# Score products on four array quarters, unread products at the start, and two stores per half group in a four-layer graph network

## The chip, the cores and the metric

The kernel runs on one core of a Trainium2 chip. The metric is the device time of one execution in microseconds (us). The program is one launch; nothing is computed on the host but the layout of the inputs.

## The reference

The input `x` holds 128 graphs of 64 nodes with 256 features; one 64x64 adjacency matrix serves them all. Four layers follow, each `x = x + layer(relu(layernorm(x)))`. Cut to what matters:

```python
# layer 0: two graph convolutions, then four LSTMs over windows of 1, 2, 3, 4 nodes
h = relu(adj @ (h @ Wg0 + bg0));  h = relu(adj @ (h @ Wg1 + bg1))
for p in 1..4: h[:, last node of each window of p] = lstm_p(windows of h)
# layer 1: spectral mix, then attention with 4 heads of 64, then an MLP
x1 = relu(layernorm((2 L / lam_max - I) @ h @ Wc + bc)) + h
q, k, v = x1 @ Wq, x1 @ Wk, x1 @ Wv            # 4 heads of 64
attn = softmax(where(adj > 0, q @ k.T / 8, -1e9))
x2 = layernorm(x1 + (attn @ v) @ Wo + bo)
x = layernorm(x2 + gelu(x2 @ W1 + b1) @ W2 + b2)
# layer 2: graph attention; layer 3: U @ (relu(U.T @ h @ W1 + b1) @ W2 + b2)
# lam_max and U come from eigenvalues and eigenvectors of 64x64 matrices
```

In layer 1 a score product is 64x64 times 64x64: one graph, one head. There are 128 x 4 of them, and as many products of probabilities and values.

## The kernel before

**Tiles.** The 128 graphs are 64 token tiles of 128 rows (two graphs each). Layer 0 goes over 8 groups of 8 tiles, layers 1 to 3 over 16 half groups of 4 tiles (`HT = 4`, 8 graphs). Features are cut into two chunks of 128 (`c`, `m`); in feature-major form a chunk holds two heads, one on partitions 0-63 and one on 64-127. All data is fp32, and each fp32 product appears in the trace as two records.

**Order.** The code records operations without emitting them (`Plan.record`). `Plan.schedule` then simulates the engines with a fixed cost per operation (`Plan.cost`), picks buffers and PSUM banks, and writes out one order for every engine. Groups have numbers: setup first, then layer 0 group by group, a set of weights loaded into the room of layer 0's weights, then the half groups of layers 1 to 3, of which several are open at once. The eigenvector work (`eig_decomp` and what follows it) is a group of its own beside layer 0: its TensorE products go ahead of all others, the rest of it behind. All records have the same line, 331, where `Plan.issue` emits; so groups are read by tiles and shapes.

**TensorE's cost in the plan.** A transpose is taken at 0.11 us, a product of at most 64 by 64 at 0.08, all others at 0.001672 us per column plus 0.006, and no less than 0.06. A list of products under `plan.burst()` is planned as one operation, at 0.3 us plus 0.036 for each product; both bursts of layer 1 have 32.

**Layer 1's two bursts.** `qT` and `kT` are feature-major: chunk `m`, and in it partition half `r`, is head `2m + r`. A score product has its contraction on the 64 partitions of half `r`. Its place in the 128x128 array is given by the half of the partitions that it reads (array rows) and the half of the partitions that it writes (array columns). Before, the scores of a head land on the partition half that the head is read from:

```python
for par, m, b in [(r, r ^ f, b) for f in range(2) for b in range(2 * HT) for r in (f, 1 - f)]:
    r = slice(par * N, par * N + N)
    PE.matmul(ps[m][r, bat(b)], qT[r, m, bat(b)], kT[r, m, bat(b)], start=True, stop=True)
```

So only the two straight quarters (0-63 to 0-63, 64-127 to 64-127) are used in each of the two passes `f`, and neighbouring products go to different banks `ps[0]`, `ps[1]`. Mask, softmax and transposes follow, on `s` and `pT`. The second burst multiplies by `v`: the graph's half of the tokens (`half`) is read, the head's half (`par`) written, in all four combinations, each half of the tokens into a bank of its own.

**The start.** `ident` and `ones` are set on chip. The first loads are `adjT`, `adj` and five pieces of `x`. Two products with `adjT` give row sums (`rsrow`), for bias tables. Then layer 0 of group 0 begins: statistics, normalised tiles `mids`, products with `adjTb`, copy, products with `Wg`.

**The end of a half group.** `layer3` adds its result to `x` in two halves of two tiles, and one store on the SyncE queue writes the four tiles (512 KB) to the output.

Of the kernel before, what the change touches and what calls it, by code (L numbers as in the profile page):

```python
# [12 lines left out]
N = 64  # L13
# [53 lines left out]
class Plan:  # L67
# [101 lines left out]
    @staticmethod  # L169
    def cost(op, aps):  # L170

        def free(ap):
            n = 1
            for _, c in ap.ap[1:]:
                n *= c
            return n
        n = max(free(a) for a in aps)
        if op.name == "dma_start" and op.eng != "SP":
            return 0.6, 4.0
        if op.eng == "PE":  # L180
            n = free(aps[0])
            if op.name == "transpose":
                c = 0.11
            elif aps[0].ap[0][1] <= 64 and aps[1].ap[0][1] <= 64:
                c = 0.08
            else:
                c = max(0.06, 0.001672 * n + 0.006)
            return c, c + 0.22
        if op.eng == "V":
            if op.name == "bn_stats":  # L190
                c = 0.33
            elif op.name == "bn_aggr":
                c = 0.09
            elif op.name in ("tensor_copy", "tensor_scalar") and all(str(a.space) == "SB" for a in aps):
                c = 0.075 + 0.0006 * n + 0.05 * (len(aps) - 2)
            elif op.name == "reciprocal":
                c = 0.075 + 0.0065 * n
            elif op.name == "tensor_reduce" and aps[1].ap[-1][0] != 1:
                c = 0.075 + 0.0022 * n
            else:  # L200
                c = 0.075 + 0.00105 * n
            if "accum_out" in op.kw:
                c += 0.075
            return c, c + 0.12
        if op.eng == "ACT":
            c = 0.07 + 0.00082 * n + 0.1 * max(0, len(aps) - 2)
            if op.kw.get("func", op.args[2] if len(op.args) > 2 else None) is AF.Exp:
                c += 0.12
            return c, c + 0.15
        if op.eng == "G":  # L210
            c = 0.44 + 0.14 * n if op.kw.get("op") is ALU.pow else 0.12 + 0.00218 * n
            return c, c + 0.05
        c = max(0.6, free(aps[0]) * aps[0].ap[0][1] * 4e-6 / 0.39)
        return c, c + 2.2
# [650 lines left out]
P = 128  # L865
D = 256
NT = 64
GT = 8
NG = NT // GT
HT = 4  # L870
# [41 lines left out]
def gnn_kernel(ctx: ExitStack, tc: tile.TileContext, a, out):  # L912
# [4 lines left out]
    def C(shape, name):  # L917
        return pool.tile(list(shape), F32, name=name)
# [40 lines left out]
    PE, V, ACT, G, SP = (plan.proxy(e) for e in ("PE", "V", "ACT", "G", "SP"))  # L959

    def bank(name):
        return plan.value("bank")
# [11 lines left out]
    xout = out.rearrange("(g t p) f -> g p t f", p=P, t=HT)  # L974
# [38 lines left out]
    V.tensor_scalar(ident, ident, 0.0, None, op0=ALU.is_equal)  # L1013
    ones = C([P, P], "ones")
    V.memset(ones, 1.0)
    mhalf = C([P, HT], "mhalf")
    V.memset(mhalf, -0.5)

# [100 lines left out]
    bat = lambda b: slice(b * N, (b + 1) * N)  # L1119

    def tm(n=HT, f=D):

        return plan.value("big")[:, :n * f].rearrange("p (t f) -> p t f", f=f)

    def fm():

        return plan.value("big")[:, :2 * HT * P].rearrange("p (c n) -> p c n", c=2)
# [168 lines left out]
    def evac(dst, src, i):  # L1296
        if i % 2:
            ACT.copy(dst, src)
        else:
            V.tensor_copy(dst, src)  # L1300
# [36 lines left out]
    def relu_norm(x):  # L1337
        sc, bi = ln_stats(x)
        h = tm()
        for t in range(HT):  # L1340
            ACT.activation(h[:, t, :], x[:, t, :], AF.Relu, scale=sc(t), bias=bi(t))
        return h
# [11 lines left out]
    def layer1(x):  # L1354
        h = relu_norm(x)
        lx = mix_fm(h, lambda t: lapb)
        x1 = tm()
        for t0 in (0, 2):
            ps = proj_tm(lambda c, t: lx[:, c, tok(t)], Wc, 2, t0)
            V.tensor_add(x1[:, t0:t0 + 2, :], ps.rearrange("p (t f) -> p t f", t=2), vec(bc, 2))  # L1360
        norm(x1)
        for t0 in (0, 2):
            xp, hp = x1[:, t0:t0 + 2, :], h[:, t0:t0 + 2, :]
            V.tensor_mul(xp, xp, vec(g1, 2))
            G.tensor_add(xp, xp, vec(be1, 2))
            V.scalar_tensor_tensor(xp, xp, 0.0, hp, op0=ALU.max, op1=ALU.add)
        x1T = to_fm(x1)
        qT, kT, v = fm(), fm(), tm()
        for m in range(2):
            evac(qT[:, m, :], proj_fm(Wq, x1T, m), 0)  # L1370
            evac(kT[:, m, :], proj_fm(Wk, x1T, m), 1)
        for t0 in (0, 2):
            evac(pair(v, t0), proj_tm(lambda c, t: x1T[:, c, tok(t)], Wv, 2, t0), 1)
        for t0 in (0, 2):
            G.tensor_add(x1[:, t0:t0 + 2, :], x1[:, t0:t0 + 2, :], vec(bo, 2))

        ps = [bank("qk") for m in range(2)]
        with plan.burst():  # L1380
            for par, m, b in [(r, r ^ f, b) for f in range(2) for b in range(2 * HT) for r in (f, 1 - f)]:
                r = slice(par * N, par * N + N)
                PE.matmul(ps[m][r, bat(b)], qT[r, m, bat(b)], kT[r, m, bat(b)], start=True, stop=True)
        s = tm(4 * HT, N)
        for m in range(2):
            sm = s[:, m * 2 * HT:(m + 1) * 2 * HT, :]
            V.scalar_tensor_tensor(sm, ps[m].rearrange("p (b k) -> p b k", k=N), 0.125, vec(mask1, 2 * HT), op0=ALU.mult, op1=ALU.add)
            stat = plan.value("stat")
            softmax_shift(sm, stat[:, :2 * HT])
            ACT.activation(sm, sm, AF.Exp)  # L1390
            ssum = stat[:, 2 * HT:4 * HT]
            V.reduce_sum(ssum, sm, axis=AX.X)
            V.reciprocal(ssum, ssum)
            G.tensor_mul(sm, sm, ssum.unsqueeze(2).to_broadcast([P, 2 * HT, N]))

        pT = fm()
        for m in range(2):
            evac(pT[:, m, :], transposes([flat(s[:, (m * HT + t) * 2:(m * HT + t) * 2 + 2, :]) for t in range(HT)]), m)
        oT = fm()

        po = [bank("o") for half in range(2)]
        with plan.burst():
            for m, t, half, par in [(m, t, half, par) for m in range(2) for t in range(HT) for half in range(2) for par in range(2)]:
                r = slice(half * N, half * N + N)
                PE.matmul(po[half][par * N:par * N + N, bat(m * HT + t)], v[r, t, bat(2 * m + par)], pT[r, m, bat(2 * t + par)], start=True, stop=True)
        for half in range(2):
            evac(oT.rearrange("p c (t b n) -> p c t b n", t=HT, b=2)[:, :, :, half, :], po[half].rearrange("p (c t n) -> p c t n", c=2, t=HT), half)
        x2 = tm()
        for t0 in (0, 2):
            ps = proj_tm(lambda c, t: oT[:, c, tok(t)], Wo, 2, t0)  # L1410
            V.tensor_add(x2[:, t0:t0 + 2, :], ps.rearrange("p (t f) -> p t f", t=2), x1[:, t0:t0 + 2, :])
        norm(x2)
        x2T = fm()
        for c in range(2):
            ACT.activation(x2T[:, c, :], transposes([x2[:, t, tok(c)] for t in range(HT)]), AF.Identity, scale=g2c[:, c:c + 1], bias=be2c[:, c:c + 1])
        V.tensor_mul(x2, x2, vec(g2))
        for t0 in (0, 2):
            G.tensor_add(x2[:, t0:t0 + 2, :], x2[:, t0:t0 + 2, :], vec(b2, 2))
        mT = [fm() for i in range(2)]
        for m in range(4):  # L1420
            ACT.activation(mT[m // 2][:, m % 2, :], proj_fm(W1, x2T, m), AF.Gelu, bias=b1[:, m:m + 1])
        for t0 in (0, 2):
            ps = proj_tm(lambda c, t: mT[c // 2][:, c % 2, tok(t)], W2, 4, t0)
            V.tensor_add(pair(x2, t0), ps, pair(x2, t0))
        for t0 in (0, 2):
            G.tensor_add(x[:, t0:t0 + 2, :], x[:, t0:t0 + 2, :], vec(be3, 2))
        norm(x2)
        for t0 in (0, 2):
            V.tensor_mul(x2[:, t0:t0 + 2, :], x2[:, t0:t0 + 2, :], vec(g3, 2))
            V.tensor_add(x[:, t0:t0 + 2, :], x[:, t0:t0 + 2, :], x2[:, t0:t0 + 2, :])  # L1430
# [55 lines left out]
    for i, g in enumerate(ORDER):  # L1486
        plan.group = REST + 2 * i
        x = X[g]
        if g < len(put):
            x = load(back[g], put[g])  # L1490
        for h in range(GT // HT):
            plan.group = REST + 2 * i + h
            xh = x[:, h * HT:(h + 1) * HT, :]
            layer1(xh)
            layer2(xh)
            layer3(xh)
            SP.dma_start(xout[g * GT // HT + h], xh)
    plan.issue()


# [51 lines left out]
```

## Time and profile before

Three runs took 2292.06, 2292.18 and 2292.21 us.

| what | value |
|---|---|
| span of the profiled execution | 2291.3 us |
| TensorE busy | 2254.4 us |
| VectorE busy | 1693.3 us |
| ScalarE busy | 969.8 us |
| GpSimd busy | 565.7 us |
| mean granted TensorE clock | 0.996 |
| table loads on ScalarE | 43, of 1.283 us each |
| stores to the output | 16 of 512 KB, median 2.9 us from issue to landing |

How to read it: busy time is the union of an engine's instructions. Where an engine is busy nearly all the time, the end moves with its work. Where it idles, the question is what it waits for. The granted clock says at which share of full speed TensorE ran. A row of the timeline gives the start, the length, the engine and the operation with its count; in square brackets stands the idle time before it and what ended it. The length of a TensorE row ends with its last product's modelled end, which overlaps the next row; the time that a row takes up is from its start to the next row's start.

### The profile page before, as it was taken

How to read it: one execution, taken by the hardware profiler on the slowest of the kernel's cores; microseconds unless marked ns; L12 is line 12 of the kernel's file. 1: busy time of each engine (PE TensorE's matmuls, PEld its weight loads, DVE VectorE, ACT ScalarE, POOL GpSimd, SP SyncE). 2: the span in 40 equal slices, each digit the busy share in tenths (PEclk: the TensorE clock that was granted, in tenths of full speed). 3: DMA queues.
4: the chain of work that ended last, by engine and by line, in shares of the span. 5: the costliest groups of instructions: out<-in, count | busy, mean ns of one | idle time of the engine just before them, and what ended most of it. 6: DMA issues, size and time to landing. Idle time of an engine off the chain costs nothing.

```text
span 2291.3 us, 33480 instructions
## 1 busy us (share of the span) xinstructions
PE 2254.4 (98%) x11288; PEld 1595.1 (70%) x11288; DVE 1693.3 (74%) x6942; ACT 969.8 (42%) x1909; POOL 565.7 (25%) x856
## 2 busy tenths in 40 slices
PE   8999999999999999999999999999999999999997
PEld 5578478468568568568568558778777776876786
DVE  6656666566899999999988723767786867767775
ACT  3333333333333333333333443455564545555672
POOL 3101001101100100100100203535374535555342
PEclk9999999999999999999999999999999999999998
DMA  7000001000000000000000011000000000000001
GB/s 247 1 1 19 0 1 38 19 1 1 1 1 1 1 1 1 1 1 1 5 1 1 9 36 31 1 1 10 20 10 10 10 28 10 28 10 1 2 19 37
DMA packets 27405, 35.48 MB, mean 15 GB/s; under 512 B 3297, under 2 KB 24673, under 8 KB 26721
## 3 DMA queue, kind: packets, MB, share of 16 engines
q1 hardware_dynamic: 26128, 32.29, 4.2%
q8 instruction: 89, 1.46, 0.3%
q10 hardware_dynamic: 1104, 1.05, 0.2%
q14 instruction: 84, 0.68, 0.1%
HBM read 22.85 MB, written 10.49 MB: 15 GB/s over the span
## 4 chain that ended last, share of the span: by engine, by line
PE 91%; DVE 5%; ACT 2%; POOL 1%; issue 1%; DMA 0%; SPq 0%; DVEq 0%; ACTq 0%
PE bank L331 91%; DVE arena L331 2%; DVE big L331 1%; DVE stat L331 1%; DVE x L331 1%; POOL stat L331 1%; ACT big L331 1%; DVE mids L331 0%; ACT arena L331 0%; ACT L331 0%; ACT mids L331 0%; ACT Wih L331 0%; DMA adj<-in_adj_dram 0%; ACT x L331 0%; DVE Whh L331 0%
## 5 line engine op out<-in xcount | busy, mean ns | idle before, releaser
L331 PE MATMUL bank<-big,Wih 128*128 128x512 f32 (+2 forms) x2640 | 887.6, 478 | 2.2 <-DVE arena L331 1.1
L331 PEld LDWEIGHTS bank<-big,Wih 128*128 128x128 f32 x2640 | 490.0, 190 | 275.3 <-issue 172.4
L331 ACT ACTIVATE mids<-bank,bl 128x256 f32<-128x256 f32 (+2 forms) x624 | 345.2, 563 | 637.0 <-PE bank L331 622.3
L331 PE MATMUL bank<-big,Whh 128*128 128x256 f32 (+3 forms) x1640 | 507.3, 444 | 0.0
L331 DVE TENSOR_TENSOR arena<-arena 64x21 f32<-64x21 f32 (+6 forms) x2316 | 375.9, 193 | 34.7 <-POOL arena L331 1.8
L331 PEld LDWEIGHTS bank<-big,Whh 128*128 128x128 f32 x1640 | 306.4, 190 | 132.4 <-issue 65.5
L331 POOL TENSOR_SCALAR stat<-stat 128x4 f32<-128x4 f32 (+1 forms) x228 | 67.5, 297 | 722.4 <-DVE stat L331 709.7
L331 DVE TENSOR_TENSOR big<-big,mids 128x256 f32<-128x256 f32 (+2 forms) x192 | 93.8, 489 | 123.7 <-ACT mids L331 122.3
L331 DVE TENSOR_TENSOR big<-mids 128x512 f32<-128x512 f32 (+2 forms) x256 | 145.9, 574 | 47.0 <-ACT mids L331 43.5
L331 ACT ACTIVATE mids<-big 128x256 f32<-128x256 f32 (+2 forms) x176 | 89.8, 510 | 99.6 <-DVE big L331 64.8
L331 PE MATMUL bank<-Wih,big 128*128 128x256 f32 (+1 forms) x560 | 130.2, 365 | 0.2 <-ACT big L331 0.2
L331 DVE TENSOR_SCALAR arena<-arena 64x1 f32<-64x1 f32 (+4 forms) x598 | 120.3, 210 | 8.2
L331 POOL TENSOR_TENSOR arena<-arena 64x1 f32<-64x1 f32 x66 | 43.6, 661 | 322.6 <-ACT arena L331 170.2
L331 POOL TENSOR_TENSOR stat<-stat,mhalf 128x4 f32<-128x4 f32 (+1 forms) x114 | 120.4, 1057 | 6.5
L331 PEld LDWEIGHTS bank<-Wih,big 128*128 128x128 f32 x560 | 97.6, 190 | 21.9 <-issue 10.7
L331 PE MATMUL bank<-Whh,big 128*128 128x256 f32 (+2 forms) x512 | 110.2, 358 | 1.4 <-DVE x L331 1.0
L331 ACT COPY big<-bank 128x512 f32<-128x512 f32 x113 | 63.0, 587 | 111.5 <-PE bank L331 94.1
L331 PEld LDWEIGHTS bank<-Whh,big 128*128 128x128 f32 (+1 forms) x512 | 82.3, 183 | 21.9 <-issue 8.3
L331 DVE COPY arena<-bank 64x1 f32<-64x1 f32 (+24 forms) x190 | 41.2, 220 | 71.4 <-PE bank L331 64.9
L331 PEld LDWEIGHTS bank<-adjTb,mids 128*128 128x128 f32 x512 | 69.8, 193 | 25.7 <-issue 17.0
L331 DVE BATCH_NORM_STATS2 stat<-x 128x6 f32<-128x256 f32 x240 | 87.2, 410 | 0.1
L331 ACT ACTIVATE mids<-x,stat 128x256 f32<-128x256 f32 x92 | 48.4, 591 | 88.2 <-POOL stat L331 88.2
(334 smaller groups left out, 3313.1 us busy)
## 6 DMA issues: line engine op xcount, KB each, us to landing
x<-in_x_dram SPq DMA_DIRECT2D x7, 1024.0 KB, 13.2
out_dram<-x SPq DMA_DIRECT2D x12, 512.0 KB, 2.9
Wih<-in_WihT_dram SPq DMA_DIRECT2D x3, 1024.0 KB, 15.7
Whh<-in_WhhT_dram SPq DMA_DIRECT2D x3, 1024.0 KB, 12.2
put<-x SPq DMA_DIRECT2D x2, 1024.0 KB, 4.4
arena<-put SPq DMA_DIRECT2D x2, 1024.0 KB, 5.9
out_dram<-arena SPq DMA_DIRECT2D x4, 512.0 KB, 3.0
Whh<-in_W_dram SPq DMA_DIRECT2D x2, 512.0 KB, 3.8
```

The lines of the kernel that those rows point to most:

```text
L331: getattr(self.engines[op.eng], name)(*map(real, args), **{k: real(a) for k, a in kw.items()})
```

## The change

It has four parts.

1. The score products of the second chunk (`m = 1`) write the other partition half (`half(r ^ m)`), so the four products of a graph lie in the four quarters of the array. They are issued graph by graph: chunk 0 with both halves into bank 0, then chunk 1 with both halves into bank 1. The second burst reads the probabilities of the second chunk at swapped places.
2. Fourteen products of `ones` with itself, 128x128, whose result nobody reads, are recorded at the beginning of the program, where TensorE has no data yet.
3. The output of a half group is stored in two halves of 256 KB.
4. The plan takes 0.2 us for a product of fewer than 128 columns, if it isn't a transpose or at most 64 by 64. The formula for wider ones stays.

```diff
             elif aps[0].ap[0][1] <= 64 and aps[1].ap[0][1] <= 64:
                 c = 0.08
             else:
-                c = max(0.06, 0.001672 * n + 0.006)
+                c = 0.001672 * n + 0.006 if n >= 128 else 0.2
...
     V.memset(ones, 1.0)
+
+    warm = bank("warm")
+    for i in range(14):
+        PE.matmul(warm[:, :P], ones, ones, start=True, stop=True)
...
         ps = [bank("qk") for m in range(2)]
+        half = lambda i: slice(i * N, i * N + N)
         with plan.burst():
-            for par, m, b in [(r, r ^ f, b) for f in range(2) for b in range(2 * HT) for r in (f, 1 - f)]:
-                r = slice(par * N, par * N + N)
-                PE.matmul(ps[m][r, bat(b)], qT[r, m, bat(b)], kT[r, m, bat(b)], start=True, stop=True)
+            for b, m, r in [(b, m, r) for b in range(2 * HT) for m in range(2) for r in range(2)]:
+                PE.matmul(ps[m][half(r ^ m), bat(b)], qT[half(r), m, bat(b)], kT[half(r), m, bat(b)], start=True, stop=True)
...
-            for m, t, half, par in [(m, t, half, par) for m in range(2) for t in range(HT) for half in range(2) for par in range(2)]:
-                r = slice(half * N, half * N + N)
-                PE.matmul(po[half][par * N:par * N + N, bat(m * HT + t)], v[r, t, bat(2 * m + par)], pT[r, m, bat(2 * t + par)], start=True, stop=True)
+            for m, t, i, r in [(m, t, i, r) for m in range(2) for t in range(HT) for i in range(2) for r in range(2)]:
+                PE.matmul(po[i][half(r), bat(m * HT + t)], v[half(i), t, bat(2 * m + r)], pT[half(i), m, bat(2 * t + (r ^ m))], start=True, stop=True)
...
-            SP.dma_start(xout[g * GT // HT + h], xh)
+            for t0 in range(0, HT, 2):
+                SP.dma_start(xout[g * GT // HT + h][:, t0:t0 + 2, :], xh[:, t0:t0 + 2, :])
```

More of the change, by code (lines that the diff above doesn't have):

```diff
@@ L1399, in layer1 @@
         oT = fm()
-        po = [bank("o") for half in range(2)]
+        po = [bank("o") for i in range(2)]
         with plan.burst():
-            for m, t, half, par in [(m, t, half, par) for m in range(2) for t in range(HT) for half in range(2) for par in range(2)]:
-                r = slice(half * N, half * N + N)
-                PE.matmul(po[half][par * N:par * N + N, bat(m * HT + t)], v[r, t, bat(2 * m + par)], pT[r, m, bat(2 * t + par)], start=True, stop=True)
-        for half in range(2):
-            evac(oT.rearrange("p c (t b n) -> p c t b n", t=HT, b=2)[:, :, :, half, :], po[half].rearrange("p (c t n) -> p c t n", c=2, t=HT), half)
+            for m, t, i, r in [(m, t, i, r) for m in range(2) for t in range(HT) for i in range(2) for r in range(2)]:
+                PE.matmul(po[i][half(r), bat(m * HT + t)], v[half(i), t, bat(2 * m + r)], pT[half(i), m, bat(2 * t + (r ^ m))], start=True, stop=True)
+        for i in range(2):
+            evac(oT.rearrange("p c (t b n) -> p c t b n", t=HT, b=2)[:, :, :, i, :], po[i].rearrange("p (c t n) -> p c t n", c=2, t=HT), i)
         x2 = tm()
```

## The prediction

> **What bounds the kernel now.** I read the page from its top: busy shares, the 40 slices, the chain that ended last. Then the timeline of TensorE where the edited instructions stand, and a table of stretches for how full TensorE is around them.
>
> ```profile
> PE 2254.4 (98%) x11288; PEld 1595.1 (70%) x11288; DVE 1693.3 (74%) x6942; ACT 969.8 (42%) x1909; POOL 565.7 (25%) x856
> PE   8999999999999999999999999999999999999997
> PE 91%; DVE 5%; ACT 2%; POOL 1%; issue 1%; DMA 0%; SPq 0%; DVEq 0%; ACTq 0%
> ```
>
> TensorE is busy in 98% of the span, in every slice but the first and the last, and 91% of the chain is its work. VectorE (74%) is next, with room. So nearly every microsecond of TensorE work removed comes off the end, and nearly every one added goes on.
>
> The two bursts of 64x64 products come next. Each fp32 product stands in the trace as two records, so 32 products are x64. One half group's scores (columns: start, duration, engine, operation, count) and another's values times probabilities, each with the row that follows:
>
> ```profile
> 2128.41 2.08 PE L331 MATMUL bank<-mids,big 64*64 64x64 f32 x64
> 2130.42 1.13 PE L331 MATMUL bank<-Whh,arena 128*128 128x256 f32 x4
> 2131.48 1.16 PE L331 MATMUL bank<-big,x 64*64 64x64 f32 x64
> 2132.57 1.13 PE L331 MATMUL bank<-Whh,arena 128*128 128x256 f32 x4
> ```
>
> From a burst's start to the next row's start: 2130.42 - 2128.41 = 2.01 us for the first kind, 2132.57 - 2131.48 = 1.09 us for the second, with equal work in them. Which is which follows from the code: the first 64x64 burst of the kernel, at 1458.74, has the long form, and scores come first; the last, at 2163.28, has the short one. The code also says why they differ: the scores before run in two quarters of the array at any time (rows 0-63 to columns 0-63 together with rows 64-127 to columns 64-127, then the two crossed quarters), the values in all four. Sixteen of each stand in the trace.
>
> How full TensorE is there (columns: stretch and length, busy us and count per engine, granted clock, DMA):
>
> ```profile
> 20.00:1458.00 1438.00, 1434.19 (x5538) 966.46 (x5537) 1075.02 (x5208) 517.37 (x1121) 155.56 (x280) 1.00 0.04 13
> 1458.00:2020.00 562.00, 553.28 (x4006) 419.72 (x4008) 420.04 (x1134) 299.22 (x534) 286.69 (x383) 1.00 0.04 13
> 2020.00:2230.00 210.00, 210.00 (x1449) 158.67 (x1442) 151.65 (x427) 128.22 (x209) 96.53 (x130) 1.00 0.02 6
> ```
>
> From 1458 to 2230 us, where all score bursts stand, TensorE idles 8.7 us of 772 (562.00 - 553.28), and none of it after 2020. VectorE works 420.0 of 562 and 151.7 of 210, so it is no second bound yet.
>
> The head, and the end of the tail:
>
> ```profile
> 9.35 2.14 PE L331 MATMUL bank<-adjTb,mids 128*128 128x128 f32 x8 [1.97 <-ACT mids L331]
> 12.17 3.47 PE L331 MATMUL bank<-Wg,mids 128*128 128x256 f32 x8 [0.68 <-ACT mids L331]
> ...
> 2286.12 1.29 DVE L331 TENSOR_TENSOR arena<-bank,arena 128x512 f32<-128x512 f32 x2 [1.72 <-PE bank L331]
> ```
>
> Eight records of 256 columns take 3.47 us (0.43 each) at 12.17; twelve take 2.81 us (0.23) at 22.47. The first ones ran at half clock. The trace states the same later, with clock 0.50 granted after TensorE had idled:
>
> ```profile
> 2233.85:2237.26 3.41, 0.82 (x8) 0.64 (x7) 3.41 (x10) 0.94 (x3) 0.00 (x0) 1.00 0.00 0
> 2237.30:2244.00 6.70, 6.03 (x28) 5.62 (x28) 4.11 (x16) 3.61 (x7) 4.69 (x9) 0.50 0.00 0
> ```
>
> **What the Trainium skill says.** "TensorEngine Tiling (Array Packing)", section Tile-to-Partition Mapping: the array splits into four 64x64 tiles, each tied to one half of the input and one half of the output partitions. The trace agrees: four quarters 1.09 us, two 2.01. "PSUM — Partial Sum Buffer", section on bank collisions: two row tiles may not write the same bank at one time; what was measured is an error per bank and quadrant of 32 partitions, and the hardware does not stall for it. This matters, since after the change rows 0-63 and rows 64-127 write one bank together, but always in different partition halves: the page's measured rule allows it, its quoted general rule doesn't. In the trace of before two row tiles never share a bank within a burst, so it shows neither. "TensorE: Matmul & The Clock Gate", Part 1: the clock is halved until about 3.4 us of sustained work, and again after an idle window; the trace agrees (above). "DMA: Bandwidth & Descriptors", Anatomy of one DMA: about 2.0 us fixed plus bytes at 436 GB/s, stated for another issuing path than this one. For 512 KB that is an estimate of 3.2 us; the trace has 2.9.
>
> **The change, part by part.**
>
> *Scores.* 32 products per half group as before, now four in flight. I take the value burst's 1.09 us as their duration, as it has the same shapes, count and four quarters: 2.01 - 1.09 = 0.92 us per burst, times 16 = 14.7 us. The values burst itself only reads its operands at swapped places for the second pair of heads: no cost. Does the saving reach the end? TensorE idles 1.1% of that stretch, so mostly; where it runs ahead of VectorE's or ScalarE's fixed order some of it becomes a wait. I take 14.0.
>
> *Fourteen unread products.* They read `ones`, set by VectorE at 0.99 us. They are 28 records at half clock: 0.21 us each (half of the 0.43 of a record twice as wide) to 0.27 (2.14 / 8), so 6.0 to 7.5 us, less if the clock rises on the way. TensorE's queue has 12 of them, then the product of `adjT` and `ones` (at 3.15 before), two more, then the one with `rscol` (6.70 before), which then waits until at most about 9. Its reader is VectorE's copy `rsrow`, at 9.01 before; behind that in VectorE's queue stand the small bias tables, and the next TensorE work at 9.35 does not need them. So they cost nothing to 0.2 us. Their gain: 2.14 us of records, and about 3 of the 3.47, ran at half clock; at full clock they take half, so at most 2.6 us. But between the unread products' end (6 to 7.5) and 9.35 TensorE is idle but for two records, and 0.82 us of work in 3.41 was followed by a halved clock at 2237. I expect the clock to be lost again in part of the cases. Bounds 0 and 2.6; I take 0.8.
>
> *Two stores.* The last store is issued at 2287.44, when both of VectorE's last additions are done; 512 KB land in 2.9 us. After it, the first half leaves one addition earlier (0.65 us, half of 1.29) and the last is of 256 KB. By the trace, 1024 KB took 4.4 and 512 KB 2.9, so 256 KB less is 0.75 us less; by the page's rate it is 0.6. I take 0.7. The sixteen extra issues cost 0.37 us each on a queue that waits most of the time; only two loads stand behind stores there, long before they are needed.
>
> *The planner's cost.* Products of under 128 columns are now planned at 0.2 us instead of 0.06 to 0.11. No instruction changes, but the written order does, from the first microseconds on. The listing of both programs' instructions by engine shows the same kinds of work but 49 table loads on ScalarE for 43 (1.28 us each in the trace, 7.7 us on an engine at 42%), and the last 846 products of TensorE in the same order of shapes: from about 2020 us on, the tail is as it was. Up to 1458 TensorE idles 3.8 us of 1438 after the head: little to win there, little to lose if the order stays as good. Between 1458 and 2020 it idles 8.7 us, and a new order can make that 5 or 14. I take 0, with 4 us either way.
>
> Sum: 14.0 + 0.8 + 0.7 = 15.5; 2292.2 - 15.5 = 2276.7 us.
>
> **The rivals.**
>
> *A, given back (2285 us).* The bursts shorten, but half of it goes into waits on VectorE and ScalarE, whose order is fixed and now has six more table loads: 6 x 1.28 = 7.7 us if all six stand in front of TensorE. For it: TensorE waited 4.6 us for `Wih` from ScalarE, waits that contain table loads. Against: between 2020 and 2230 it idles not at all. 2276.7 + 7.7 = 2284.4, about 2285.
>
> *B, no overlap gained (2291 us).* Rows 0-63 and 64-127 in one bank hold each other up, so two of the four run at a time, as before: 2.01 us stay. Only head and tail remain: 2292.2 - 1.5 = 2290.7. For it: the page's quoted rule. Against: its measured one.
>
> *C, slower (2320 us).* The four products run one at a time. Two quarters take 2.01 us, so one takes about twice the streaming part: the four to two step costs 0.92 us for 16 slots, the two to one step 32 slots, 1.84 us. Times 16 = 29.4; with B's 2290.7 that is 2320.1. A badly placed new order would end on this side too. Against: in the trace the crossed quarters of the scores already alternate row tiles without that cost.
>
> **How the numbers follow.** Forecast 0.70, A 0.15, B 0.08, C 0.07. The forecast's own spread: 14.7 fully realised, 2.6 at the head and 4 from order would make 2270; I go to 2269 below. Above, 2290 takes in A and nearly reaches B; that holds all but about 0.05 of the forecast, most of A and some of B: 0.8. Faster by over 0.2% means below 2287.6: the forecast with A, less what of A falls above, 0.84. Within: B and that rest, 0.09. Slower: C, 0.07.
>
> **What would show it.** Right: the score bursts' next row starts 1.1 us after them, sixteen times; TensorE's busy time falls by 14 to 15 us while its idle time between 1458 and 2230 stays near 8.7; the records at 9.35 take about half of 2.14 us or the full; the last store lands about 2.2 us after its issue. Wrong: bursts of 2.0 us (B) or 3.9 (C); idle time in the middle grown by over 5 us (A); or TensorE waits before 1458 that were not there.

## The result and the profile after

Six runs of the changed kernel took 2276.39 us in the median (2273.3 to 2277.03); the kernel before, run beside it, 2292.40 us. The ratio is 0.9928, with a 95% interval of 0.9915 to 0.9940. The forecast was 2276.7 us.

The page of the changed kernel; first busy time and share per engine, then TensorE's 40 slices, then the chain that ended last:

```profile
PE 2244.4 (99%) x11316; PEld 1585.8 (70%) x11316; DVE 1685.7 (74%) x6942; ACT 977.3 (43%) x1915; POOL 564.0 (25%) x856
PE   9999999999999999999999999999999999999997
PE 91%; DVE 5%; ACT 2%; POOL 1%; issue 1%; DMA 0%; SPq 0%; DVEq 0%; ACTq 0%
```

TensorE stays the bound: 99% busy, the same 91% of the chain. It is busy 10 us less in a span 16.5 us shorter, although 28 records (the unread products) are new. The busy total alone doesn't give the parts, since it counts those records too. They take 4.88 + 0.71 = 5.6 us (in the head, below); the prediction's sign, a fall of 14 to 15 us, had left them out.

The bursts of one half group in the timeline of TensorE (start, duration, engine, operation, count):

```profile
2010.63 1.16 PE L331 MATMUL bank<-mids,big 64*64 64x64 f32 x64
2011.73 1.16 PE L331 MATMUL bank<-lapb,Whh 128*128 128x128 f32 x8
2012.82 1.16 PE L331 MATMUL bank<-x,arena 64*64 64x64 f32 x64
2013.91 0.94 PE L331 MATMUL bank<-lapb,Whh 128*128 128x128 f32 x6
```

From start to the next row's start both bursts now take 1.1 us; the scores took 2.01. Read one by one, the 64 records of the first score burst start in groups, about 58 ns from one group to the next for most of the burst: groups of two before, of four after. The same stretches as before (length, busy us and count per engine, granted clock, DMA):

```profile
20.00:1458.00 1438.00, 1435.65 (x5545) 968.18 (x5544) 1075.53 (x5212) 516.76 (x1123) 154.53 (x283) 1.00 0.04 13
1458.00:2020.00 562.00, 552.90 (x4138) 419.02 (x4137) 425.01 (x1156) 313.80 (x550) 292.22 (x390) 1.00 0.04 14
2020.00:2230.00 210.00, 206.74 (x1379) 155.14 (x1378) 151.98 (x439) 129.26 (x211) 98.04 (x135) 0.99 0.02 6
```

The middle stretch has 132 records more in the same 562 us, with no less idle time: 9.1 us, 8.7 before. In the third stretch the waits of 2.6 and 0.7 us at the start of the tail, at 2237 and 2239 before, have moved inside (210.00 - 206.74 = 3.26 us), since the kernel is shorter.

The head of the changed kernel, and the granted clock (the column before the last two) in four stretches:

```profile
1.03 4.88 PE L331 MATMUL bank<-ones 128*128 128x128 f32 x24 [1.03 <-DVE ones L331]
5.84 0.43 PE L331 MATMUL bank<-adjT,ones 64*128 64x64 f32 x2
6.21 0.71 PE L331 MATMUL bank<-ones 128*128 128x128 f32 x4
7.12 0.43 PE L331 MATMUL bank<-adjT,rscol 64*128 64x64 f32 x2 [0.20 <-DVE rscol L331]
9.77 2.14 PE L331 MATMUL bank<-adjTb,mids 128*128 128x128 f32 x8 [2.21 <-ACT mids L331]
12.59 3.78 PE L331 MATMUL bank<-Wg,mids 128*128 128x256 f32 x8 [0.67 <-ACT mids L331]
```

```profile
5.20:8.50 3.30, 2.15 (x15) 1.63 (x13) 2.04 (x11) 0.00 (x0) 1.19 (x5) 1.00 0.94 269
8.60:18.70 10.10, 8.26 (x27) 6.99 (x28) 6.54 (x39) 3.76 (x7) 5.74 (x16) 0.50 0.92 323
2223.80:2227.10 3.30, 3.30 (x15) 3.30 (x16) 2.92 (x13) 1.05 (x3) 2.47 (x6) 0.50 0.00 0
2240.90:2247.60 6.70, 6.03 (x28) 6.03 (x29) 2.17 (x5) 3.39 (x7) 4.11 (x6) 0.50 0.00 0
```

The trace's entries on the clock begin at 5.1 us, with 1.00; the unread records start 0.21 us apart up to there and 0.11 us apart behind it. So the clock rose on them. From 8.5 to 18.8 us it is 0.50 again. It fell about 1 us into the idle time of 2.21 us. The prediction reads from the trace of before that the clock falls after an idle window; here TensorE was busy for 2.15 of the 3.30 us before the fall (the row 5.20:8.50). The first eight records take 2.14 us, as before, the next eight 3.78 (3.47 before). In this execution the head gained nothing.

### The profile page after: what moved, and what is told of

It is laid out like the page before. It is cut to its first block, busy times and chain, and to the rows that moved or that the text cites. A ratio compares the mean times of both kernels' runs of the same rounds, so it can differ in the third digit from the quotient of the medians.

```text
span 2274.8 us, 33569 instructions
## 1 busy us (share of the span) xinstructions
PE 2244.4 (99%) x11316; PEld 1585.8 (70%) x11316; DVE 1685.7 (74%) x6942; ACT 977.3 (43%) x1915; POOL 564.0 (25%) x856
## 3 DMA queue, kind: packets, MB, share of 16 engines
q10 hardware_dynamic: 1104, 1.05, 0.2%
## 4 chain that ended last, share of the span: by engine, by line
PE 91%; DVE 5%; ACT 2%; POOL 1%; issue 1%; DMA 0%; SPq 0%; DVEq 0%; ACTq 0%
PE bank L331 91%; DVE arena L331 1%; DVE stat L331 1%; DVE big L331 1%; DVE x L331 1%; POOL stat L331 1%; ACT arena L331 1%; DVE mids L331 0%; ACT mids L331 0%; ACT big L331 0%; DMA adj<-in_adj_dram 0%; ACT x L331 0%; ACT Wih L331 0%; DVE Whh L331 0%; POOL x L331 0%
## 5 line engine op out<-in xcount | busy, mean ns | idle before, releaser
L331 PE MATMUL bank<-big,Wih 128*128 128x256 f32 (+2 forms) x2592 | 865.1, 476 | 0.9 <-DVE arena L331 0.3
L331 PEld LDWEIGHTS bank<-big,Wih 128*128 128x128 f32 x2592 | 481.6, 190 | 268.4 <-issue 165.9
L331 PE MATMUL bank<-big,Whh 128*128 128x256 f32 (+3 forms) x1704 | 538.0, 450 | 0.0
L331 PEld LDWEIGHTS bank<-big,Whh 128*128 128x128 f32 x1704 | 319.3, 191 | 140.3 <-issue 74.6
L331 DVE TENSOR_SCALAR arena<-arena 64x1 f32<-64x1 f32 (+5 forms) x596 | 117.1, 204 | 8.4
L331 PE MATMUL bank<-Wih,big 128*128 128x256 f32 (+1 forms) x520 | 117.6, 362 | 1.2 <-ACT big L331 1.2
L331 PEld LDWEIGHTS bank<-Wih,big 128*128 128x128 f32 x520 | 90.9, 190 | 20.2 <-issue 8.6
L331 PEld LDWEIGHTS bank<-adjTb,mids 128*128 128x128 f32 x512 | 70.8, 196 | 26.7 <-issue 17.5
L331 DVE SCALAR_TENSOR_TENSOR arena<-arena 64x1 f32<-64x1 f32 (+4 forms) x389 | 77.2, 205 | 10.5 <-POOL arena L331 4.1
L331 POOL MEMSET arena<- 64x2 f32 (+5 forms) x72 | 8.0, 113 | 309.2 <-DVE arena L331 309.1
L331 PE MATMUL bank<-adjTb,mids 128*128 128x128 f32 x512 | 73.6, 282 | 3.0 <-ACT mids L331 2.9
```

The costliest lines, as they stand in the source:

```text
L331: getattr(self.engines[op.eng], name)(*map(real, args), **{k: real(a) for k, a in kw.items()})
```

## The experiments

Each was run beside the kernel before on the same chip; the medians of the kernel before there were 2291.84 to 2293.33 us. `e1` to `e4` share a chip, so do `e5` to `e8`, and `e9` to `e11`. The interval of a ratio is about 0.001 either way; that of the difference of two such ratios is an estimated 0.0016, or 3.7 us, from those of `e2_no_scores` and the changed kernel.

**Each part alone**

`e1_scores` puts the score part of the diff into the kernel before. Every engine keeps its order.

> The score part alone, put into the kernel before; every engine keeps the order of before, only the 16 score bursts differ. Theory 1 (the shorter bursts pass on whole): each burst takes 1.09 us from its start to the next row's start, 2.01 before; 16 x 0.92 = 14.7 us less, 2277 to 2279 us. Theory 2 (part of it becomes waits on VectorE and ScalarE, and the new order of the whole change made up for it): 2282 to 2286 us, with TensorE's idle time between 1458 and 2230 us grown from 8.7 us to over 12.

Measured: 2280.27 us, ratio 0.9949 (0.9937 to 0.9962): 11.6 us less than the 2291.89 of the kernel before. Nearly all its bursts take 1.09 us; the 32 bursts of both kinds hold TensorE 35.2 us (49.6 before). The time lies between the two theories. Two views of this kernel, the stretch from 1458 to 2020 and whom TensorE waited for from 1458 to 2010 (total us, times, longest):

```profile
1458.00:2020.00 562.00, 551.49 (x4129) 417.10 (x4128) 427.82 (x1148) 303.88 (x541) 290.98 (x387) 1.00 0.04 13
```

```profile
PE bank L331 <- DVE x L331: 2.1, 3, 1.0
PE bank L331 <- ACT Wih L331: 2.1, 2, 1.5
PE bank L331 <- DVE arena L331: 2.0, 3, 1.2
PE bank L331 <- ACT big L331: 1.9, 5, 0.7
```

The idle time is 10.5 us where before has 8.7. With the two smaller lines of that view the waits are 8.6 us, 6.8 before; VectorE's `arena` went from 1.2 in one wait to 2.0 in three. So 1.8 of the 14.7 us became waits in that stretch. The 43 table loads of before are unchanged here, so rival A's six new ones are not the reason here.

`e2_no_scores` is the changed kernel with the two bursts of before, in the changed kernel's order.

> The whole change without its score part: unread products, two stores and the planner's cost, in the order of the changed kernel. Theory 1: what remains is the store's 0.7 us and what head and order bring, 2289 to 2292 us. Theory 2: the new order is worth several us by itself, 2282 to 2287 us.

Measured: 2286.12 us, ratio 0.9972 (0.9961 to 0.9982), 5.8 us less than before. Theory 2. From here to the changed kernel the scores bring 9.7 us (2286.12 - 2276.39, on two chips; by ratios 0.0044, 10.1 us).

`e3_cost` has the planner's new line alone, `c = 0.001672 * n + 0.006 if n >= 128 else 0.2`.

> The planner's new cost for narrow products alone: only the written order changes, with 49 table loads on ScalarE in place of 43. Theory 1: within 4 us of before either way (2288 to 2296), since TensorE idles 12.5 us in all between 20 and 2020 us. Theory 2: 5 us or more faster (under 2287.5).

Measured: 2290.11 us, ratio 0.9992 (0.9984 to 1.0000), 1.8 us less: within the bound of theory 1.

`e4_stores` has the two stores alone. By the traces TensorE's order moves here too.

> The two stores alone. Theory 1: the last store is of 256 KB and lands 2.2 us after its issue in place of 2.9: 0.7 us less, 2291.7 us, plus or minus what the slightly moved order does (under 2 us). Theory 2 (the landing of the last store is hidden or the extra issue costs it): 2292.4 us as before.

Measured: 2292.22 us, ratio 0.9999 (0.9991 to 1.0007). The median can't tell 0.7 us here, as its runs spread over 4.8 us. The trace can. For the output tensor, issue to landing:

```profile
DMA to landing us min/median/max: 2.1/2.3/4.1
```

The view of before has 2.9/2.9/4.3 there. From the start of TensorE's last record to the end of the span it is 5.28 us before, 4.58 with two stores: 0.70 us.

`e5_warm` has the 14 unread products alone.

> The 14 unread products alone (the order moves too, since they hold a bank and TensorE in the plan). Theory 1: the clock rises on them and is lost again while TensorE idles until the first data, in most executions; 2291 to 2293 us, with executions of up to 2.6 us less where it is kept. Theory 2 (the clock stays up): 2289 to 2290 us in all executions.

Measured: 2292.83 us (2290.42 to 2294.59), ratio 1.0002 (0.9994 to 1.0011). No gain, as theory 1. Read by tiles and shapes, its other TensorE records stand in the order of before, so nothing here is hidden by a new order. In the profiled execution, which was the fastest, the wait before the first data is 1.20 us and the first eight records take 1.50 us; from 10.6 us on the clock is 0.50 again. It is also halved again, for 6.8 us, in the profiles of `e2_no_scores`, `e7_two_passes` and `e8_row_bank`, which have the same unread products.

**What the bursts need**

`e7_two_passes` keeps the four quarters of the changed kernel but issues chunk by chunk:

```diff
-for b, m, r in [(b, m, r) for b in range(2 * HT) for m in range(2) for r in range(2)]:
+for b, m, r in [(b, m, r) for m in range(2) for b in range(2 * HT) for r in range(2)]:
```

> The changed kernel with its four quarters, but issued chunk by chunk: first the straight quarters for all eight graphs, then the crossed ones. Everything else stands as in the changed kernel. Theory 1 (the gain is that four quarters are in flight at a time, which the order of issue decides): bursts of 2.01 us, 14.7 us slower than the changed kernel, about 2291 us. Rival (the places alone are enough, the queue looks ahead): 1.09 us and 2276 us.

Measured: 2285.92 us (0.9970, interval 0.9958 to 0.9982), 9.5 us above the changed kernel and 9.9 above `e8_row_bank` on the same chip. A score burst of it with the row behind it:

```profile
1457.79 1.91 PE L331 MATMUL bank<-mids,Whh 64*64 64x64 f32 x64
1459.63 1.56 PE L331 MATMUL bank<-Wih,big 128*128 128x256 f32 x6
```

1459.63 - 1457.79 = 1.84 us; over sixteen bursts that is 16 x (1.84 - 1.09) = 12.0 us, of which 9.5 arrive. Theory 1 in kind, somewhat smaller in size: with the places alone most of the gain is gone, so it hangs on the order of issue. The 0.17 us under 2.01 come from the middle of the burst: there some records of the two chunks start together. Before, both passes used the same two quarters, and no records of the two passes do.

`e8_row_bank` gives each half of the array's rows its own bank:

```diff
-PE.matmul(ps[m][half(r ^ m), bat(b)], qT[half(r), m, bat(b)], ...
+PE.matmul(ps[r][half(m), bat(b)], qT[half(r), m, bat(b)], ...
-... pT[half(i), m, bat(2 * t + (r ^ m))] ...
+... pT[half(i), r, bat(2 * t + m)] ...
```

> The changed kernel with each half of the array's rows writing a bank of its own (bank r, partition half m), so that no two row halves write one bank at a time; the second burst reads its probabilities accordingly. Theory 1 (row halves in one bank but in different partition halves don't hold each other up): bursts of 1.09 us and 2276 us, as the changed kernel. Rival (they cost a little in each burst): bursts under 1.05 us and 1 us or more off.

Measured: 2276.06 us, ratio 0.9930 (0.9917 to 0.9944). Its first burst takes 1.09 us too:

```profile
1457.68 1.16 PE L331 MATMUL bank<-mids,Whh 64*64 64x64 f32 x64
1458.77 1.56 PE L331 MATMUL bank<-Wih,big 128*128 128x256 f32 x6
```

So two row halves writing one bank, in different partition halves, cost nothing that can be seen. This agrees with what the Trainium skill, "PSUM — Partial Sum Buffer", section on bank collisions, gives as measured (per bank and quadrant of partitions), and not with the wider rule that it quotes. Rival B of the prediction is out.

**Order and head**

`e10_skip` plans the changed kernel with the unread products and leaves them out when the instructions are written (`plan.drop = list(plan.ops[-14:])`, skipped in `issue`).

> The changed kernel in its own order, planned with the 14 unread products but with these left out when the instructions are written. Theory 1 (the clock raised by them is mostly lost before the first data): within 1 us of the changed kernel, 2276 to 2277.5 us. Rival (they bring up to 2.6 us): 2278 to 2279 us.

Measured: 2275.99 us, ratio 0.9922 (0.9909 to 0.9934). The unread products of the changed kernel bring nothing that can be measured.

`e11_no_warm` leaves them out of the plan too, which was to give a third order.

> The changed kernel without the 14 unread products in the plan too, so that the order is another one. Theory 1 (the order drawn by the plan is worth several us, by chance): apart from e10_skip by 1 to 4 us, 2277 to 2281 us (the 2290.1 us of the new planner's cost alone, less 11.6 for the scores and 0.7 for the stores, is 2277.8). Rival (orders are alike, the gain of 5.8 us without the scores came from the head): as e10_skip.

Measured: 2275.32 us, ratio 0.9922 (0.9908 to 0.9935). Not apart from `e10_skip`. But the order isn't another one: read by tiles and shapes, all 11288 TensorE records of `e10_skip` and of `e11_no_warm` stand in the sequence of the changed kernel without its unread ones. So this run tests neither the theory nor the rival; it is `e10_skip` once more.

`e12_no_warm_no_scores` is that kernel with the bursts of before. By the traces its order is that of `e2_no_scores`, without the unread products.

> The kernel of e11_no_warm with the scores of before, in the same order on every engine: the third order in which the score part is taken alone (11.6 us in the order of before, 9.7 in that of the changed kernel, by medians). Theory 1 (how much of the 14.7 us arrives depends on the waits of that order, and this one has fewer): 13 to 15 us slower than e11_no_warm, 2288 to 2290.5 us. Rival (about 10 us arrive in any order): 2285 to 2286.5 us.

Measured: 2288.16 us, ratio 0.9980 (0.9971 to 0.9989). The scores bring 12.8 us (by ratios 0.0058, 13.3). That is at the lower edge of theory 1, but theory 1's reason, a third order with fewer waits, falls: it is the order in which they brought 9.7 above. With 3 to 4 us either way, 10.1, 11.7 (`e1_scores`) and 13.3 us are not told apart.

**Filling the idle time**

`e6_fill` adds ten unread products in the gap before the first data:

```diff
+    for i in range(10):
+        PE.matmul(warm[:, :P], ones, rscol.to_broadcast([P, P]), start=True, stop=True)
     rsrow = C([P, 2, 2, N], "rsrow")
```

> The changed kernel with 10 more unread products behind the row-sum product with rscol (they read rscol, so they can't run earlier), in the gap before the first data; the other engines keep the order of the changed kernel. Theory 1 (the clock is lost in that gap): now it stays up in nearly all executions, the eight records of the first adjTb products take 1.1 us in place of 2.1 and the first Wg products 1.9 in place of 3.5 to 3.8; 1.5 to 3 us less than the changed kernel, 2273 to 2275 us. Rival (the clock at the head is not what sets the start of the full stream, the data are): 2276 us as the changed kernel.

Measured: 2273.51 us (2271.99 to 2274.09), ratio 0.9917 (0.9904 to 0.9931). `e8_row_bank`, the nearest to the changed kernel on the same chip, took 2275.51 to 2277.49. The head:

```profile
7.94 2.50 PE L331 MATMUL bank<-rscol,ones 128*128 128x128 f32 x20
10.28 1.05 PE L331 MATMUL bank<-adjTb,mids 128*128 128x128 f32 x8
12.01 1.99 PE L331 MATMUL bank<-Wg,mids 128*128 128x256 f32 x8 [0.68 <-ACT mids L331]
```

The first data records take 1.05 and 1.99 us in place of 2.14 and 3.78, and the first score burst starts at 1455.8, at 1458.9 in the changed kernel: 3.1 us. By the medians it is 2.5 us on the same chip (2276.06 - 2273.51).

`e9_tail` adds to that 8 and 12 unread products in the last two half groups, behind the product with `same`:

```diff
+        if plan.group >= REST + 14:
+            idle = bank("idle")
+            for i in range(12 if plan.group > REST + 14 else 8):
+                PE.matmul(idle[:, :P], same, flat(s2d)[:, :P], start=True, stop=True)
```

> The kernel of e6_fill with 8 and 12 more unread products in the last two half groups, behind layer 2's product with same, where TensorE waits 2.6 and 3.8 us on the last half groups' chains. Theory 1 (an idle stretch near the end costs twice, since the clock is halved after it): clock 0.50 for at most one stretch of 3.4 us after 2200 us in place of 10.2 us in the changed kernel, and 1 to 3 us less than e6_fill, 2270.5 to 2272.5 us. Rival (the tail is set by the chain through VectorE and ScalarE, TensorE's clock doesn't matter there): 2273.5 us as e6_fill.

Measured: 2270.67 us (2269.51 to 2274.05), ratio 0.9903 (0.9890 to 0.9917), the fastest of all. On the same chip `e10_skip` took 2275.99 and `e11_no_warm` 2275.32. The tail of it, and of the changed kernel:

```profile
2213.00:2268.00 55.00, 45.09 (x299) 39.80 (x297) 33.02 (x96) 18.25 (x36) 16.23 (x26) 1.00 0.14 48
```

```profile
2214.00:2274.00 60.00, 46.01 (x268) 40.85 (x266) 34.74 (x104) 18.36 (x36) 16.65 (x27) 0.91 0.13 44
```

The clock stays at 1.00, where it was 0.91 in the mean. Against `e6_fill` the gain is not clear of the intervals.

## Why the prediction was right, point by point

The sum was right within 0.3 us, in part by luck: the scores brought less than was taken, and the order, taken as nothing, made up for it.

*Scores, 14.7 us of work.* Shown: the 32 bursts of both kinds hold TensorE 34.8 us in the changed kernel, 49.6 before, and the difference is 14.8 us. One reading of the code was wrong. The prediction says that the scores before ran first in the two straight quarters, "then the two crossed quarters", and uses this against rival C. By the code both passes used the straight ones, and each half of the rows wrote the other bank in the second pass. Two at a time it was all the same, so the 2.01 us and the forecast of 1.09 stand.

*14.0 of it at the end.* Too much. By medians it was 11.6 in the order of before (`e1_scores`), and 9.7 and 12.8 in that of the changed kernel (with and without the unread products). The prediction argued from 1.1% of idle time that nearly all would pass. The profiles show where the rest went. One row starts with the 400th record from the end of TensorE's work, ahead of the tail's long waits; here it is in `e2_no_scores` and in the changed kernel:

```profile
2199.99 1.03 PE L331 MATMUL bank<-Wih,big 128*128 128x256 f32 x4
2189.21 1.03 PE L331 MATMUL bank<-Wih,big 128*128 128x256 f32 x4
```

| without the new scores | with them | row without | row with | earlier by |
|---|---|---|---|---|
| before | `e1_scores` | 2203.91 | 2191.68 | 12.2 |
| `e2_no_scores` | changed kernel | 2199.99 | 2189.21 | 10.8 |
| `e12_no_warm_no_scores` | `e11_no_warm` | 2200.26 | 2186.36 | 13.9 |

Two of these need a correction. In the first pair the stream starts 0.8 us later with the scores (one product with `adjTb` at 17.5 and 18.3 us), and the profile of before holds a halved clock that costs 1.7 us (below): 12.2 + 0.8 - 1.7 = 11.3. In the second it starts 0.4 us later (the same product at 18.6 and 19.0): 10.8 + 0.4 = 11.2. So between 11.2 and 13.9 us arrive at this row, and the rest became waits. Waits of TensorE from 1458 to 2020 (2009 or 2010 for the shorter kernels) without and with the scores are 6.8 and 8.6 us, 5.6 and 7.7, 5.7 and 6.3. One wait of the changed kernel, with the idle time in brackets:

```profile
1875.79 0.61 PE L331 MATMUL bank<-lapb,x 128*128 128x128 f32 x4
1877.79 0.44 PE L331 MATMUL bank<-ident,mids 128*128 128x128 f32 x2 [1.39 <-ACT mids L331]
```

In `e10_skip`, with the same order, the same row comes without a wait:

```profile
1874.75 0.61 PE L334 MATMUL bank<-lapb,x 128*128 128x128 f32 x4
1875.19 0.38 PE L334 MATMUL bank<-ident,mids 128*128 128x128 f32 x2
```

The reason stands two engines back. ScalarE's `mids` waits for `stat` from GpSimd, and that one instruction takes 2.46 us in the changed kernel and 0.66 in `e10_skip`; first the changed kernel, then `e10_skip`:

```profile
1874.64 2.46 POOL L331 TENSOR_SCALAR stat<-stat 128x4 f32<-128x4 f32 x1
1877.13 2.08 ACT L331 ACTIVATE mids<-mids,stat 128x256 f32<-128x256 f32 x4 [1.97 <-POOL stat L331]
1873.60 0.66 POOL L334 TENSOR_SCALAR stat<-stat 128x4 f32<-128x4 f32 x1
1874.29 2.08 ACT L334 ACTIVATE mids<-mids,stat 128x256 f32<-128x256 f32 x4 [0.16 <-POOL stat L334]
```

In `e2_no_scores` it takes 0.23 us, which is the median of the 220 instructions of this kind. The long one runs beside two pairs of additions of VectorE (1874.53 to 1877.01) and ends just behind them; what holds it up was not tested. So the other engines' fixed order is a part of the account, and their timing against each other is another.

Behind the row of the table stands the tail. In `e10_skip` it takes 79.4 us from the row to the start of the last TensorE record, in `e11_no_warm` 83.0, with the same records. What differs is the clock (column before the last two), first `e10_skip`, then `e11_no_warm`:

```profile
2186.40:2266.10 79.70, 69.09 (x402) 59.43 (x400) 52.76 (x159) 35.75 (x64) 27.69 (x44) 0.96 0.10 34
2186.40:2270.00 83.60, 73.13 (x402) 63.02 (x400) 53.12 (x159) 35.80 (x64) 27.65 (x44) 0.90 0.10 32
```

So a single execution moves by some 3.7 us there, and medians of five to eleven runs do not tell 9.7 from 12.8.

*Order, taken as 0 with 4 either way.* Without the scores the change is worth 5.8 us (`e2_no_scores`), 0.7 of it the store and nothing seen from the head (`e10_skip`), so about 5 is order. The same order without the unread products has 4.7 - 0.7 = 4.0 (2292.88 - 2288.16, less the store). So it lies at the bound. The new cost alone gives 1.8, and the stores alone, whose order differs too, give nothing. The traces show about half of it: the waits after 1458 are 1.2 us less in `e2_no_scores` than before (5.6 for 6.8), those from 20 to 1458 1.4 less (idle 2.4 for 3.8), 2.6 in all. The profile of before also has a halved clock behind a wait for `Wih`:

```profile
1891.55 0.66 PE L331 MATMUL bank<-ident,Wih 128*128 128x128 f32 x4 [1.54 <-ACT Wih L331]
1892.35 3.65 PE L331 MATMUL bank<-Whh,Whh 128*128 128x512 f32 x4
```

```profile
1892.60:1895.80 3.20, 3.20 (x5) 1.12 (x5) 2.70 (x16) 1.85 (x4) 1.98 (x4) 0.50 0.02 5
```

Halved over 3.4 us, it costs half of that, 1.7. But this can't be put down to the order: `e5_warm`, whose other records stand in the order of before, has the same wait and keeps its clock.

```profile
1891.77 0.66 PE L331 MATMUL bank<-ident,Wih 128*128 128x128 f32 x4 [1.54 <-ACT Wih L331]
1892.57 1.98 PE L331 MATMUL bank<-Whh,Whh 128*128 128x512 f32 x4
```

The rest of the 4 to 5 us stays open. That the six more table loads would cost something (rival A) was wrong in sign.

*Head, 0.8.* About nothing. The reason held: the clock is lost again around the first data. The sign named for it, "about half of 2.14 us or the full", fitted either outcome. `e6_fill` shows that keeping it is worth 2.5 to 3.1 us, at or a little over the bound of 2.6.

*Store, 0.7.* 0.70 in the trace. The unread products cost nothing that can be measured, and the values burst neither, as predicted.

*Rivals.* B and C are out: bursts of 1.09 us, with one bank for both row halves or two. A happened in part, by waits but not by its table loads, and was outweighed.

## What to carry to other kernels

Here small products used four quarters of the array at a time only when products for different quarters were neighbours in the order of issue: the same places, issued in two passes, kept most of the cost (1.84 us of 2.01). Where TensorE is 98% busy, work taken from it still doesn't arrive whole at the end: between two thirds and nine tenths did here by the medians, and a new order alone moved the time by 2 to 5 us. Compare one row ahead of the tail in two traces before explaining a difference of a few microseconds: the tail alone differed by 3.7 us between two runs of the same order. The unread products kept TensorE's clock where they reached up to the first data; those that ended 2.2 us earlier brought nothing.

## What was not expected of the hardware

In the tail an idle TensorE is followed by a halved clock. TensorE idles 10.5 us after 2200 us in the changed kernel, and its clock is 0.50 there for 10.2 us. With 20 unread products in the two longest waits the idle time is 6.4 us and the clock stays at 1.00. Filling the waits saves nothing by itself; the gain is the clock. The time fell from 2273.51 to 2270.67 us (two chips; by ratios from 0.9917 to 0.9903, with intervals that overlap). In which stretches the clock is halved differs between executions of the same order (`e10_skip` and `e11_no_warm` above), and the time goes with it: of the 28 runs of the kernel before beside `e1_scores`, the fastest (2288.91 us) has a mean clock of 0.998, the slowest (2294.94) one of 0.996.
